# Where an engine reads its ids, and the order of the last scalings, in a gated adapter with layer norm

## The chip, the cores and the metric

The kernel runs on one core of one Trainium2 chip. The metric is the device time of one execution in microseconds (us); the number that counts is the median of a few executions. TensorE (PE), VectorE (DVE), ScalarE (ACT), GpSimd (POOL) and SyncE (SP) each work through an instruction list of their own, in order. SP issues almost all DMA transfers here.

## The reference

Each of 128 batches holds a matrix x of 128 rows and 512 columns in float32 and one id from 0 to 8 (the tables have ten rows). The id picks a small network out of ten, and the result is added to x:

```
h   = relu(x @ W1[id] + b1[id])               # 128x512 @ 512x128
y   = x + h @ W2[id] + b2[id]                 # 128x128 @ 128x512
n   = (y - mean(y)) / sqrt(var(y) + 1e-5)     # per row of 512
out = x + n * gamma[id] + beta[id]
```

The ids are known only on the chip, so every table address depends on a value that an engine has to read into one of its registers.

## The kernel before, in words

One batch is one tile of 128x512, and all 128 batches go through the same steps, about seven of them in flight at once. For batch b:

- SP loads x two batches at a time (`load_x`, L188) and stores the result two at a time (`store`, L632). The tables W1 (as 128x512 tiles), W2, and the broadcast rows of beta, gamma and b2 stay in SBUF. The early batches load their W1 from HBM (`load_first`, L326); from batch 17 on ACT mostly copies it in SBUF (`stage_w1`, L481), and some batches load it (`load_rows`, L453, `load_late`, L742).
- PE transposes x in four blocks (`transpose_x`, L490), ACT copies the result to SBUF (`copy_xT`, L494), PE multiplies with W1 (`down`, L513, eight matmul records), ACT applies the relu (`relu`, L521), PE multiplies with W2 (`up`, L535, two records).
- GpSimd makes x + b2 (`add_b2`, L500) and x + beta (`add_beta`, L507). DVE adds x + b2 to the product and sums the rows (`residual`, L553); ACT squares and sums (`square`, L576), forms the negative mean (`scalar_means`, L567) and the root (`deviation`, L586); DVE refines the root in three small steps (`rstd`, L590, L592, L595), multiplies y - mean by gamma (`scale`, L619) and ends with times rstd plus x + beta (`finish`, L628).

The order on each engine is written out. After a written-out opening, a list `plan` holds every step of the middle with a position: the batch number plus an offset out of the tables `STEPS`. The list is sorted by position and issued; `keep` chains the instructions of one engine in that order. A position one higher is about 2.2 us later. Behind the plan stands a closing list, written out step by step, for the last batches: with E = 123, E+2, E+3 and E+4 are batches 125, 126 and 127.

**Reading ids.** `read_ids` (L271) issues one register read (TENSOR_LOAD in the profile) that brings a few ids from an SBUF row into registers of one engine. The ids of the first 20 batches (`NEAR`) lie unpacked in `lang` and are read four at a time (`near`); the other 108 lie packed, four batches to a word, in the 27 words of `packed`, read four words at a time and three the last time (`far`). A group is read once per engine, at the first call that needs it; later calls use the registers. GpSimd reads all 27 packed words in one go (`far_at_once`, called at L793). Before the change, PE reads groups 0 and 4 of `lang` in the opening (L773); the other reads stand in the plan as steps of their own:

- `lid` of batch b+5 on ACT and PE and of b+6 on GpSimd, at position b+0.99 (L819 to L822); only the first call for a group reads;
- on DVE group b+4 behind the scaling of every fourth batch (L865);
- the seven groups of `packed` on ACT, PE and DVE at 6.5, 6.3 and 7.0 and every two positions after that (L869 to L871), so the last ones stand at 18.5, 18.3 and 19.0.

SP reads its groups where it needs them, and that is not touched.

**The closing list.** For the last five batches the steps are taken apart: `mean_of` (L670 on ACT), `square_of` (L688), `root_of` (L586), `rstd_of` (L590, L592, L595), `scale` (L619) or `scale_out` (L719, the same product into another tile), `end_of` (L713, the last sum), and for batch 125 a sum on PE: `diag_of` (L729 on ACT), `product_of` (L734), `copy_out` (L737 on ACT). `store_last` (L745 on SP) stores single batches and halves; SP takes them in the order of the list.

Of the kernel before, what the change touches and what calls it, by code (L numbers as in the profile page):

```python
# [13 lines left out]
ET = mybir.EngineType  # L14
# [3 lines left out]
G = 4  # L18
# [125 lines left out]
def cond_resid_kernel(ctx: ExitStack, tc: tile.TileContext, x, itok, W1, b1, W2, b2, gamma, beta, out):  # L144
# [8 lines left out]
    nc = tc.nc  # L153
# [9 lines left out]
    def keep(ins):  # L163

        engine = ins.ins.engine
        if engine in last:
            tc.add_manual_dep(ins.ins, last[engine], behind, reason="kept order")
        last[engine] = ins.ins.name
        return ins
# [14 lines left out]
    E = B - 5  # L184
# [70 lines left out]
    NEAR, BITS = 20, 5  # L255
    FAR = (B - NEAR) // 4
# [13 lines left out]
    def read_ids(tile, engine, most, why):  # L270
        loads, vals = nc.values_load_multi_w_load_instructions(  # L271
            tile, engines=[engine], min_val=0, max_val=most, skip_runtime_bounds_check_because=why
        )
        for ins in loads:
            keep(ins)
        return vals

    def near(b, engine):
        g = b // G
        if (g, engine) not in lids:  # L280
            lids[g, engine] = read_ids(
                lang[0:1, g * G : (g + 1) * G], engine, L - 1, "clamped on the chip to 0..L-1 above"
            )
        return lids[g, engine][b % G]
# [13 lines left out]
    def far_at_once(engine):  # L298
        vals = read_ids(packed, engine, ((1 << 4 * BITS) - 1) * H, "four ids of 0..L-1 at five bits each, times H")
        for i in range(0, FAR, G):  # L300
            lids[(NEAR + i) // G, engine] = vals[i : i + G]
# [200 lines left out]
    def add_beta(b):  # L502
        g, j = divmod(b, 2)
        if g not in os:
            os[g] = op.tile([P, 2, H], FP, tag="o", name=f"o_{g}")
        v = lid_h(b, ET.Pool)
        keep(nc.gpsimd.tensor_tensor(os[g][:, j, :], xb(b), beta_b[:, bass.ds(v, H)], ALU.add))  # L507
# [108 lines left out]
    def scale(b):  # L616
        v = lid_h(b, ET.DVE)
        keep(
            nc.vector.scalar_tensor_tensor(  # L619
                ys[b], ys[b], col(nmeans, b), gamma_b[:, bass.ds(v, H)], ALU.add, ALU.mult  # L620
            )
        )
# [43 lines left out]
    def mean_of(b, engine):  # L666
        if b // 2 not in nmeans:
            nmeans[b // 2] = st.tile([P, 2], FP, tag="nmean", name=f"nmean_{b // 2}")
        if engine is nc.scalar:
            keep(nc.scalar.activation(col(nmeans, b), col(sums, b), AF.Copy, scale=-1.0 / H))  # L670
        else:
            keep(
                nc.vector.scalar_tensor_tensor(  # L673
                    col(nmeans, b), col(sums, b), -1.0 / H, ys[b][:, 0:1], ALU.mult, ALU.bypass
                )
            )
# [4 lines left out]
    def add_of(b, cols=slice(0, H)):  # L681
        o = out_of(b)[:, cols]
        keep(nc.gpsimd.tensor_tensor(o, rs[b][:, cols], o, ALU.add))

    def square_of(b):
        ssqs[-b] = st.tile([P, 1], FP, tag="ssq", name=f"ssq_of_{b}")
        sq = tp.tile([P, H], FP, tag="sq", name=f"sq_{b}", bufs=1)
        keep(nc.scalar.activation(sq, ys[b], AF.Square, bias=col(sums, b), scale=-float(H), accum_out=ssqs[-b]))  # L688
# [6 lines left out]
    def rstd_of(b, n):  # L695
        t, u = parts_of[-b]
        if n < 3:
            newton(n, ssqs[-b], t, u)
        else:
            rstds[-b] = st.tile([P, 1], FP, tag="rstd", name=f"rstd_of_{b}")  # L700
            newton_3(rstds[-b], t, u)
# [3 lines left out]
    def base_of(b, pool, tag):  # L705
        base[b] = pool.tile([P, H], FP, tag=tag, name=f"base_{b}")
        pick_b = pick[:, bass.ds(lid(b, ET.PE), 1)].to_broadcast([96, P])
        keep(nc.tensor.matmul(base[b], lhsT=pick_b, rhs=parts[:96, :], start=True, stop=False))
        keep(nc.tensor.matmul(base[b], lhsT=ident, rhs=xb(b), start=False, stop=True))

    def end_of(b, cols=slice(0, H)):
        o = out_of(b)[:, cols]
        keep(nc.vector.scalar_tensor_tensor(o, (rs if b in base else ys)[b][:, cols], rstd_col(b), base[b][:, cols] if b in base else o, ALU.mult, ALU.add))  # L713

    def scale_out(b):
        v = lid_h(b, ET.DVE)
        rs[b] = rp.tile([P, H], FP, tag="r", name=f"n_{b}")
        keep(
            nc.vector.scalar_tensor_tensor(  # L719
                rs[b], ys[b], col(nmeans, b), gamma_b[:, bass.ds(v, H)], ALU.add, ALU.mult  # L720
            )
        )
# [3 lines left out]
    def diag_of(b, engine):  # L726
        diags[b] = st.tile([P, P], FP, tag="diag", name=f"diag_{b}", bufs=2)
        if engine is nc.scalar:
            keep(nc.scalar.activation(diags[b], ident, AF.Identity, scale=rstd_col(b)))  # L729
        else:  # L730
            keep(nc.vector.tensor_scalar(diags[b], ident, rstd_col(b), None, ALU.mult))
# [12 lines left out]
    def store_last(b, engine=nc.sync, cols=slice(0, H)):  # L744
        keep(engine.dma_start(out=out[b][:, cols], in_=os[b // 2][:, b % 2, cols]))  # L745
# [45 lines left out]
    spread(18, nc.scalar)  # L791
    spread(19, nc.scalar)
    far_at_once(ET.Pool)  # L793
    add_beta(0)
    add_beta(1)
    spread(20, nc.scalar)
# [13 lines left out]
    def at(when, step, *args):  # L810
        plan.append((when, len(plan), step, args))

    def when(name, b):
        return b + of(STEPS[name], b)

    for b in range(B):
        if b >= 20 and b % X == 0:
            at(b + X_STEPS[b // X - 10], load_x, b // X)
        if b >= 3:  # L819
            for n, engine in ((b + 5, ET.Activation), (b + 5, ET.PE), (b + 6, ET.Pool)):  # L820
                if n < NEAR:
                    at(b + 0.99, lid, n, engine)  # L822
        if turn(b) in "Fw":
            at(when("load", b), load_rows if turn(b) == "F" else load_late, b)
        if turn(b) == "F":
            at(when("load", b), load_blocks, b)
            at(when("turn", b), turn_blocks, b)
        elif 5 <= b <= E - 2:
            at(when("transpose", b), transpose_x, b)
            at(when("copy", b), copy_xT, b)  # L830
        if 4 <= b <= E - 3:
            if b2_on_gpsimd(b):
                at(when("r", b), add_b2, b)
            at(when("beta", b), add_beta, b)
            at(when("down", b), down, b)
            at(when("relu", b), relu, b)
        if seeded(b):
            at(when("seed", b), seed, b)
        if FIRST <= b <= E - 1 and turn(b) not in "Fw":
            at(when("w1", b), stage_w1, b)  # L840
        if 2 <= b <= E - 4:
            at(when("up", b), up, b)
# [4 lines left out]
    def at_pair(g, key, step, *args):  # L847
        if g < E // 2 - 3 or (step, *args) in begun:
            at(key, step, *args)

    for g in range(E // 2 - 1):
        b = 2 * g
        for n in (b, b + 1):
            if b2_by_vector(n):
                at_pair(g, when("vb2", n), vector_b2, n)
            at_pair(g, when("stat", n), residual, n)
            at_pair(g, when("square", n), square, n)
        at_pair(g, when("means", b), scalar_means, g)
        at_pair(g, when("root", b), deviation, g)
        for n in (1, 2, 3):  # L860
            at_pair(g, when(f"n{n}", b), rstd, g, n)
        for n in (b, b + 1):
            at_pair(g, when("scale", n), scale, n)
            at_pair(g, when("end", n), finish, n)
        if b % G == 0 and b + G < NEAR:  # L865
            at_pair(g, when("scale", b) + 0.001, lid, b + G, ET.DVE)
        at_pair(g, when("store", b), store, g)

    for n in range(0, FAR, G):  # L869
        for engine, first in ((ET.Activation, 6.5), (ET.PE, 6.3), (ET.DVE, 7.0)):  # L870
            at(first + n / 2, far, NEAR + n, engine)  # L871

    for _, _, step, args in sorted(plan, key=lambda step: step[:2]):
        step(*args)
# [119 lines left out]
    root_of(E + 3)  # L994
    rstd_of(E + 2, 3)
    square_of(E + 4)
    diag_of(E + 2, nc.scalar)
    scale_out(E + 2)
    base_of(E + 2, p_y, "y")
    root_of(E + 4)  # L1000
    mean_of(E + 4, nc.scalar)
    rstd_of(E + 3, 1)
    base_of(E + 4, p_y, "y")
    rstd_of(E + 3, 2)
    add_of(E + 1, halves[0])
    rstd_of(E + 3, 3)
    product_of(E + 2)
    store_last(E + 1, nc.sync, halves[1])
    scale(E + 3)
    rstd_of(E + 4, 1)  # L1010
    store_last(E + 1, nc.sync, halves[0])
    end_of(E + 3)
    rstd_of(E + 4, 2)
    rstd_of(E + 4, 3)
    copy_out(E + 2)
    scale_out(E + 4)
    store_last(E + 3, nc.sync)
    end_of(E + 4, halves[1])
    store_last(E + 2, nc.sync)
# [40 lines left out]
```

## Time and profile before

| | |
|---|---|
| time, median of 3 executions | 301.47 us (300.65, 301.47, 301.47) |
| the profiled execution, own time | 300.83 us |
| its span, first to last instruction | 299.1 us |
| granted TensorE clock | 0.996 |
| busy share of the span: PE, DVE, ACT, POOL | 97%, 97%, 91%, 92% |
| HBM read and written | 51.71 MB and 33.55 MB, 285 GB/s over the span |

Times in the rows count from the first instruction of the span. A row of the timeline begins with start and duration in us, then engine, line, operation, tiles and the number of merged instructions; in square brackets stands the idle time of the engine before it and what ended it. An engine with a q behind its name (PEldq, DVEq, SPq) is the engine's sequencer: register reads, semaphore waits and DMA issues stand there and do not count as busy. A row of a source line gives the shortest, median and longest duration in ns and the first and last start in us.

### The profile page before, as it was taken

What the parts mean: (1) busy time and instruction counts of PE and PEld (TensorE: products, weight loads), DVE (VectorE), ACT (ScalarE), POOL (GpSimd) and SP (SyncE); (2) the same over time, 40 slices, a digit from 0 to 9 for tenths busy, and PEclk for the clock granted to TensorE, in tenths of its full rate; (3) what the DMA queues carried; (4) which work ended last, traced back from release to release, by engine and by line L of the source; (5) the groups of instructions that cost most, each with busy time, mean ns of one, the idle gap of its engine ahead of it and who ended that gap; (6) DMA issues with size and microseconds to landing.
All of it is one profiled execution on the core that took longest, in us unless ns stands there. A gap on an engine that the chain in (4) does not pass through costs nothing. (4 is left out here: it accounts for less than half of the span.)

```text
span 299.1 us, 8487 instructions
## 1 busy us (share of the span) xinstructions
PE 290.8 (97%) x1779; PEld 216.3 (72%) x1779; DVE 288.9 (97%) x780; ACT 273.4 (91%) x760; POOL 276.3 (92%) x238
## 2 busy tenths in 40 slices
PE   7999998999999999999999999999999999999992
PEld 3868776777777777777777777777777777777760
DVE  6999998999999999999999999999999999999995
ACT  4877886999999999999999999999999999899992
POOL 1199998998999999999999999999999999999982
PEclk9999999999999999999999999999999999999998
DMA  6999999989487997869995997859976898993816
GB/s 228 384 388 369 343 312 407 360 287 286 168 279 245 312 390 229 317 206 345 323 301 179 276 403 249 323 191 328 346 226 253 277 355 265 307 346 121 272 50 234
DMA packets 62260, 85.82 MB, mean 287 GB/s; under 512 B 4185, under 2 KB 26212, under 8 KB 62210
## 3 DMA queue, kind: packets, MB, share of 16 engines
q1 hardware_dynamic: 62150, 85.23, 83.8%
q8 instruction: 16, 0.26, 0.4%
q14 instruction: 34, 0.28, 0.3%
q10 hardware_dynamic: 60, 0.05, 0.1%
HBM read 51.71 MB, written 33.55 MB: 285 GB/s over the span
## 5 line engine op out<-in xcount | busy, mean ns | idle before, releaser
L507 POOL TENSOR_TENSOR o<-x,beta_b 128x512 f32<-128x512 f32 x121 | 153.6, 1304 | 12.6 <-DVE beta_b L408 12.6
L513 PEld LDWEIGHTS ph<-xT,w1s 128*128 128x128 f32 x1024 | 126.9, 192 | 15.1 <-ACT hT L521 9.1
L513 PE MATMUL ph<-xT,w1s 128*128 128x128 f32 x1024 | 135.7, 275 | 1.2 <-ACT sq L576 1.1
L500 POOL TENSOR_TENSOR r<-x,b_b 128x512 f32<-128x512 f32 x83 | 106.7, 1305 | 2.9 <-DVE part L592 2.2
L535 PE MATMUL py<-w,hT 128*128 x196 | 100.5, 595 | 0.0
L490 PEld LDWEIGHTS pxT<-ident,x 128*128 128x128 f32 x464 | 60.2, 151 | 52.5 <-issue 38.0
L619 DVE SCALAR_TENSOR_TENSOR py<-py,nmean,gamma_b 128x512 f32<-128x512 f32 x124 | 92.5, 751 | 0.3
L576 ACT ACTIVATE sq<-py,sum 128x512 f32<-128x512 f32 x124 | 86.1, 694 | 2.8 <-DVE py L553 1.0
L628 DVE SCALAR_TENSOR_TENSOR o<-py,rstd,o 128x512 f32<-128x512 f32 x116 | 84.9, 746 | 2.7 <-issue 1.5
L494 ACT COPY xT<-pxT 128x512 f32<-128x512 f32 x116 | 68.3, 588 | 7.9 <-PE pxT L490 6.5
L490 PE MATMUL pxT<-ident,x 128*128 128x128 f32 x464 | 71.3, 277 | 0.1
L553 DVE SCALAR_TENSOR_TENSOR py<-py,r 128x512 f32<-128x512 f32 x88 | 60.7, 690 | 0.0
L521 ACT ACTIVATE hT<-ph,b1T 128x128 f32<-128x128 f32 x128 | 47.7, 373 | 4.8 <-PE ph L513 2.4
L481 ACT COPY w1s<-w 128x512 f32 x80 | 48.7, 622 | 0.2
L535 PEld LDWEIGHTS py<-w,hT 128*128 128x128 f32 x196 | 30.1, 192 | 1.8 <-issue 1.1
L527 PE MATMUL py<-w,hT 128*128 x60 | 30.8, 595 | 0.0
L576 ACT ACTIVATION_READ_ACCUMULATOR sq<-py,sum 128x1 f32 x124 | 25.9, 209 | 0.0
L553 DVE SCALAR_TENSOR_TENSOR py<-py,b_b 128x512 f32<-128x512 f32 x30 | 20.6, 687 | 0.0
L473 ACT COPY py<-x 128x512 f32<-128x512 f32 x30 | 18.0, 599 | 0.2 <-DVE o L628 0.2
L586 ACT ACTIVATE root<-ssq,eps 128x2 f32<-128x2 f32 x62 | 16.9, 273 | 0.5
L567 ACT ACTIVATE nmean<-sum 128x2 f32<-128x2 f32 x61 | 13.0, 213 | 0.3 <-DVE rstd L595 0.2
L553 DVE DVE_READ_ACCUMULATOR py<-py,r 128x1 f32 x88 | 12.3, 139 | 0.0
(83 smaller groups left out, 152.9 us busy)
## 6 DMA issues: line engine op xcount, KB each, us to landing
x<-in_x_dram SPq DMA_DIRECT2D x64, 512.0 KB, 7.3
out_dram<-o SPq DMA_DIRECT2D x62, 512.0 KB, 6.7
w1s<-in_L_cond_W_dram SPq DMA_DIRECT2D x25, 256.0 KB, 7.3
w1s<-in_L_cond_W_dram SPq DMA_DIRECT2D x48, 64.0 KB, 4.1
x<-in_x_dram SPq DMA_DIRECT2D x48, 64.0 KB, 2.0
w<-in_L_cond_W_dram SPq DMA_DIRECT2D x4, 640.0 KB, 8.1
w<-in_L_cond_W_dram SPq DMA_DIRECT2D x1, 1792.0 KB, 9.9
w<-in_L_cond_W_dram SPq DMA_DIRECT2D x1, 768.0 KB, 5.3
```

The source lines that it names most:

```text
L481: keep(nc.gpsimd.tensor_copy(dst, src) if gpsimd else nc.scalar.copy(dst, src))
L490: keep(nc.tensor.transpose(pxs[b][:, k, :], cols, ident))
L494: keep(nc.scalar.copy(xT[b], pxs.pop(b)))
L500: keep(nc.gpsimd.tensor_tensor(rs[b], xb(b), b2_b[:, bass.ds(v, H)], ALU.add))
L507: keep(nc.gpsimd.tensor_tensor(os[g][:, j, :], xb(b), beta_b[:, bass.ds(v, H)], ALU.add))
L513: nc.tensor.matmul(phs[b], lhsT=w1s[b][:, k, :], rhs=xT_of(b, k), start=(k == 0), stop=(k == KC - 1))
L521: keep(nc.scalar.activation(hT[b], phs.pop(b), AF.Relu, bias=b1T[:, bass.ds(lid(b, ET.Activation), 1)]))
L535: keep(nc.tensor.matmul(ys[b], lhsT=hT[b], rhs=w2[:, bass.ds(v, H)], start=not m, stop=True))
L553: nc.vector.scalar_tensor_tensor(ys[b], ys[b], 1.0, r, ALU.mult, ALU.add, accum_out=sum_of(b))
L576: nc.scalar.activation(sq, ys[b], AF.Square, bias=col(sums, b), scale=-float(H), accum_out=col(ssqs, b))
L619: nc.vector.scalar_tensor_tensor(ys[b], ys[b], col(nmeans, b), gamma_b[:, bass.ds(v, H)], ALU.add, ALU.mult)
L628: nc.vector.scalar_tensor_tensor(o, ys[b], rstds[g][:, j : j + 1], o, ALU.mult, ALU.add)
```

## The change

The reads of ids move. GpSimd reads its five groups of `lang` right behind the packed words, in the opening. On ACT, PE and DVE the eleven groups behind the first stand in one row in the plan, from positions 3.9, 3.7 and 4.1 on, 0.55 apart, so the last ones stand at 9.4, 9.2 and 9.6. The three sets of read steps in the plan go away. The number of reads on each engine stays.

In the closing list the negative mean of batch 127 (ACT) moves ahead of the diagonal of batch 125, directly behind the square of 127; the scaling of 126 (DVE) moves ahead of the three root steps of 126; the scaling of 127 (DVE) moves ahead of the second root step of 126 and of all those of 127; and the three root steps of 126 and 127 are interleaved ahead of the last sum of 126.

```diff
@@ opening @@
     far_at_once(ET.Pool)
+    for n in range(0, NEAR, G):
+        near(n, ET.Pool)
     add_beta(0)
@@ plan, for b in range(B) @@
-        if b >= 3:
-            for n, engine in ((b + 5, ET.Activation), (b + 5, ET.PE), (b + 6, ET.Pool)):
-                if n < NEAR:
-                    at(b + 0.99, lid, n, engine)
@@ plan, for g in range(E // 2 - 1) @@
-        if b % G == 0 and b + G < NEAR:
-            at_pair(g, when("scale", b) + 0.001, lid, b + G, ET.DVE)
         at_pair(g, when("store", b), store, g)
 
-    for n in range(0, FAR, G):
-        for engine, first in ((ET.Activation, 6.5), (ET.PE, 6.3), (ET.DVE, 7.0)):
-            at(first + n / 2, far, NEAR + n, engine)
+    reads = [(near, n) for n in range(0, NEAR, G)] + [(far, NEAR + n) for n in range(0, FAR, G)]
+    for n, (read, b) in enumerate(reads[1:]):
+        for engine, first in ((ET.Activation, 3.9), (ET.PE, 3.7), (ET.DVE, 4.1)):
+            at(first + n * 0.55, read, b, engine)
@@ closing list @@
     square_of(E + 4)
+    mean_of(E + 4, nc.scalar)
     diag_of(E + 2, nc.scalar)
     scale_out(E + 2)
     base_of(E + 2, p_y, "y")
     root_of(E + 4)
-    mean_of(E + 4, nc.scalar)
+    scale(E + 3)
     rstd_of(E + 3, 1)
     base_of(E + 4, p_y, "y")
+    scale_out(E + 4)
     rstd_of(E + 3, 2)
     add_of(E + 1, halves[0])
+    rstd_of(E + 4, 1)
     rstd_of(E + 3, 3)
     product_of(E + 2)
     store_last(E + 1, nc.sync, halves[1])
-    scale(E + 3)
-    rstd_of(E + 4, 1)
+    rstd_of(E + 4, 2)
     store_last(E + 1, nc.sync, halves[0])
+    rstd_of(E + 4, 3)
     end_of(E + 3)
-    rstd_of(E + 4, 2)
-    rstd_of(E + 4, 3)
     copy_out(E + 2)
-    scale_out(E + 4)
     store_last(E + 3, nc.sync)
     end_of(E + 4, halves[1])
     store_last(E + 2, nc.sync)
```

## The prediction

> **What bounds the kernel now.** I read the page first, then the busy time by stretches, then the waits, then the reads of ids by their own source line, which the page leaves out because register reads do not count as busy.
>
> ```profile
> 18.00:31.00 13.00, 12.93 (x78) 9.82 (x77) 12.28 (x30) 9.90 (x29) 13.00 (x11) 1.00 1.07 370
> 43.00:53.00 10.00, 8.84 (x54) 6.13 (x53) 8.46 (x23) 7.41 (x20) 8.91 (x8) 1.00 1.05 390
> 53.00:278.00 225.00, 224.90 (x1422) 170.54 (x1420) 223.80 (x593) 219.56 (x619) 223.14 (x188) 1.00 0.84 282
> ```
>
> Each row gives a stretch, its length, and the busy time of PE, PE's weight loads, DVE, ACT and GpSimd. From 53 to 278 us PE idles 0.10 us of 225, DVE 1.20, GpSimd 1.86, ACT 5.4: nothing there can make up for lost time, since three engines are full at once. So time lost before 53 us should still be missing at 278, and time saved should still be saved. The one stretch with a hole is 43 to 53: PE, DVE and GpSimd each lose over 1 us. The timeline of that hole, engine by engine:
>
> ```profile
> 49.33 0.60 PE L490 MATMUL pxT<-ident,x 128*128 128x128 f32 x4
> 51.02 1.13 PE L513 MATMUL ph<-xT,w1s 128*128 128x128 f32 x8 [1.08 <-ACT sq L576]
> 49.20 0.37 ACT L521 ACTIVATE hT<-ph,b1T 128x128 f32<-128x128 f32 x1
> 49.97 0.69 ACT L576 ACTIVATE sq<-py,sum 128x512 f32<-128x512 f32 x1
> 52.03 0.59 ACT L494 COPY xT<-pxT 128x512 f32<-128x512 f32 x1 [1.28 <-issue]
> 50.32 0.69 DVE L553 SCALAR_TENSOR_TENSOR py<-py,r 128x512 f32<-128x512 f32 x1
> 52.54 0.75 DVE L628 SCALAR_TENSOR_TENSOR o<-py,rstd,o 128x512 f32<-128x512 f32 x1 [1.47 <-issue]
> ```
>
> PE's wait is put down to ACT's square, which the matmul of L513 doesn't use. The last thing that it uses, the relu that frees its bank, ended at 49.20 + 0.37 = 49.57. By the plan, the step that stands at each of the three holes is the last read of packed ids: on PE between the transposes and L513 (position 18.3), on ACT between the square and the copy (18.5), on DVE between the residual and the finish (19.0). The source line of the reads, first from 17 to 43 us, then from 43 to 53:
>
> ```profile
> L271 PEldq TENSOR_LOAD <-packed x5: 329/330/333, 22.1 to 39.5; - x5
> L271 ACTq TENSOR_LOAD <-packed x5: 305/310/310, 23.3 to 39.4; - x5
> L271 DVEq TENSOR_LOAD <-packed x5: 338/342/351, 24.4 to 41.1; - x5
> L271 DVEq TENSOR_LOAD <-lang x4: 340/374/598, 18.6 to 40.7; - x4
> ...
> L271 PEldq TENSOR_LOAD <-packed x2: 1253/1686/2119, 43.3 to 48.8; - x2
> L271 ACTq TENSOR_LOAD <-packed x2: 997/1631/2265, 44.2 to 49.7; - x2
> L271 DVEq TENSOR_LOAD <-packed x2: 885/1554/2224, 47.7 to 50.2; - x2
> L271 DVEq TENSOR_LOAD <-lang x1: 789/789/789, 49.2 to 49.2; - x1
> ```
>
> From 17 to 41 us the fifteen reads of packed ids take 0.31 to 0.35 us, and those of `lang` on DVE 0.37 in the middle (its first 0.60); the seven reads behind 43 us take 0.79 to 2.27. The last read on PE starts at 48.8 and takes 2.12, so it ends at 50.96, and L513 starts at 51.02; on ACT and DVE the read ends 0.1 us ahead of the next instruction as well. So the holes are slow reads. What makes them slow, the rows show only by its time: SP's first result store is issued in between.
>
> ```profile
> 40.91 0.41 SPq L632 DMA_DIRECT2D out_dram<-o  x1
> ```
>
> **The change part by part.**
>
> *The reads leave the slow stretch.* Their new positions, 3.7 to 9.6, lie between PE's transposes of batch 5 (3.90) and the matmul of batch 8 (9.09), which the rows below have at 20.49 and 29.38; so the last read falls near 30 us, over 10 us ahead of the first store, where the rows above have reads of 0.33. PE's L513 could then start when the transposes have issued. Normal pitches:
>
> ```profile
> 20.49 0.64 PE L490 MATMUL pxT<-ident,x 128*128 128x128 f32 x4
> ...
> 27.16 1.06 PE L513 MATMUL ph<-xT,w1s 128*128 128x128 f32 x8
> 28.05 1.02 PE L535 MATMUL py<-w,hT 128*128 x2
> 28.91 0.64 PE L490 MATMUL pxT<-ident,x 128*128 128x128 f32 x4
> 29.38 1.06 PE L513 MATMUL ph<-xT,w1s 128*128 128x128 f32 x8
> ...
> 43.69 1.02 PE L535 MATMUL py<-w,hT 128*128 x2
> 44.80 1.13 PE L513 MATMUL ph<-xT,w1s 128*128 128x128 f32 x8
> ```
>
> The pitch from transposes to L513 is 0.47 (28.91 to 29.38), so L513 comes at 49.33 + 0.47 = 49.80 instead of 51.02: 1.22 us. The first slow PE read, at 43.3, makes the pitch behind L535 1.11 instead of 0.86: 0.25 more. Together PE gets 1.47. DVE would start its finish at about 50.98 instead of 52.54, 1.56, and ACT gets 1.28. Late next are PE and ACT about equally; ACT has 5.4 us of idle time in the next stretch and takes the smaller number without harm. I take 1.4 for the steady stretch; the ends are 1.2 (the large hole on PE alone) and 1.56 (DVE's).
>
> *The reads arrive in a full stretch.* From 18 to 31 us PE is at 12.93 of 13 and DVE at 12.28, and by about 30 us five reads more on PE and eight more on DVE run there than before. Each takes 0.33 to 0.34 on the sequencer, which runs ahead of the engine: the read costs nothing while the instruction in front still works. PE's pieces between two reads are 0.47, 0.89 or 0.86 long, DVE's large ones 0.69 and more; the shortest cover is longer than a read. Only on DVE do two reads stand behind one instruction (0.68 against 0.69 of a residual). If the cover is gone, a read costs at most its own 0.34; for eight that is 2.7 us. The nearest rows are the reads of the same stretch, around which PE lost 0.07 us in all, so I take 0.1, between 0 and 2.7.
>
> The Trainium skill, "DMA: Bandwidth & Descriptors", section "Latency and other measured facts", speaks against this move: it gives a register load (`tensor_load`) a floor of about 600 ns. By that floor the ten reads on PE would not fit under a cover of 0.47 us, and the sum would be 1.3 us worse; the rows here have 0.33 and disagree with it.
>
> *GpSimd.* Four reads of 0.32 move from behind running adds to the opening, where GpSimd waits for the beta rows. It reads the first group at 9.5, so the four more end near 11, and its first add starts at 14.07.
>
> ```profile
> L271 POOLq TENSOR_LOAD <-lang x5: 322/324/343, 9.5 to 31.3; - x5
> ...
> 14.07 4.98 POOL L507 TENSOR_TENSOR o<-x,beta_b 128x512 f32<-128x512 f32 x4 [12.60 <-DVE beta_b L408]
> ...
> 69.62 1.27 POOL L500 TENSOR_TENSOR r<-x,b_b 128x512 f32<-128x512 f32 x1 [1.13 <-DVE part L592]
> ```
>
> They cost nothing under the 12.6 us of idle time, and gain nothing, as the adds in front hid them. If GpSimd were the bound, the saving would die in it, because it idles only 1.86 us behind 53. But 1.13 of these are one wait on DVE, at 69.62, which shrinks by what DVE gains, so GpSimd can follow by 1.13; the other 0.3 has to come out of its lead, and the view of waits behind 53 has no row in which DVE or PE waits for GpSimd.
>
> *The closing list.*
>
> ```profile
> 291.27 0.75 DVE L719 SCALAR_TENSOR_TENSOR n<-py,nmean,gamma_b 128x512 f32<-128x512 f32 x1
> 292.23 0.39 ACT L729 ACTIVATE diag<-ident,rstd_of 128x128 f32<-128x128 f32 x1
> 291.93 0.16 DVE L590 SCALAR_TENSOR_TENSOR part_of<-ssq_of,root_of 128x1 f32<-128x1 f32 x1
> 292.59 0.76 DVE L619 SCALAR_TENSOR_TENSOR py<-py,nmean,gamma_b 128x512 f32<-128x512 f32 x1
> 292.71 0.19 ACT L670 ACTIVATE nmean<-sum 128x1 f32<-128x1 f32 x1
> 293.38 0.75 DVE L713 SCALAR_TENSOR_TENSOR o<-py,rstd_of,o 128x512 f32<-128x512 f32 x1
> 294.50 0.75 DVE L719 SCALAR_TENSOR_TENSOR n<-py,nmean,gamma_b 128x512 f32<-128x512 f32 x1
> 295.37 0.87 DVE L713 SCALAR_TENSOR_TENSOR o<-n,rstd_of,base 128x256 f32<-128x256 f32 x2
> 294.16 0.33 SPq L745 DMA_DIRECT2D out_dram<-o  x1
> 296.30 0.38 SPq L745 DMA_DIRECT2D out_dram<-o  x1
> DMA to landing us min/median/max: 1.9/2.0/2.7
> ```
>
> On the old clock: the scaling of 126 can start behind L719 of 125, at 291.93 instead of 292.59; one root step; the scaling of 127 at about 292.66 instead of 294.50 (its mean takes the diagonal's place at 292.23 and is there at 292.4 instead of 292.9); five small steps, some 0.19 apart where they depend on each other, to 293.9; the last sum of 126 at 293.9 instead of 293.38, later by 0.5; the two halves of 127 from 294.56 instead of 295.37, earlier by 0.8. ACT's diagonal starts 0.1 later, and the sum of 125 with it. The end is a store, and SP issues them in order: 126 at about 294.68 instead of 294.16, then 125, then the halves, about 0.42 to 0.47 apart. The last issue comes at about 296.0 instead of 296.30. So of 0.8 on DVE the late start of 126's store eats most; 0.3 is left at the issue. The store of 126, 256 KB, now lands nearer to the others, so I take 0.25; the ends are -0.2 (the four stores share one stretch of transfer) and 0.8 (DVE's gain in full).
>
> *Sum:* 1.4 - 0.1 + 0.25 = 1.55, from the profiled execution's 300.83 (span 299.1, and 1.7 around it): 299.3. This execution is 0.64 under the median of the three runs, 301.47; for half of that I add 0.3: **299.6**.
>
> **The rivals.** *The saving dies in a full engine.* GpSimd is 99% busy behind 53, and if its wait at 69.62 doesn't shrink, DVE runs into it, and only the tail and a part of the hole is left: about 300.4. For it speaks GpSimd's 13.00 of 13.00 from 18 to 31 and 223.14 of 225.00 behind 53; against it, that the waits name no engine that waits for it behind 53.
>
> *The reads stay slow where they go.* The rows tie slowness to the time behind 41 us, not to the store. If full DMA queues make it, the early stretch, where the DMA share is 1.07 as against 1.05 in the hole, could have slow reads too. At 0.60, the longest read there so far, PE's ten reads would outlast their shortest cover of 0.47 by 0.13 each, 1.3 in all, and most of the saving would be gone: 299.6 + 1.3 = 300.9. This is also the case in which the change does not do what it says. Against it stand the fifteen reads at 0.31 to 0.35. The Trainium skill's floor of 600 ns leads to the same time.
>
> *Slower: uncovered reads.* It decides itself at a cover shorter than 0.34 us. If DVE's eight more reads all stood in the open, 2.7 us would be lost before 31 us and never made up: 300.83 - 1.4 - 0.25 + 2.7 = 301.9, and 302 with the runs' median.
>
> *More than forecast.* If DVE's hole and all of the tail on DVE count, 1.56 + 0.8 = 2.4 is saved: 298.5.
>
> **How the numbers follow.** Forecast 0.66, more 0.08, dies in an engine 0.14, slow reads early 0.07, uncovered reads 0.05. A measurement of this kernel can tell about 0.3% from no change, which is 0.9 us, so the line lies at 300.57. Faster: 0.66 + 0.08 + a fifth of the third case = 0.77; within: 0.18; slower: 0.05. The range goes from 298.6, near the largest saving, to 300.9, which takes in the case of a full engine and the early slow reads.
>
> **What would show it.** Right: all reads of PE, ACT and DVE end by 31 us and take about 0.33; no idle time by issue near 50 us; the wait of GpSimd near 69 is gone or shrunk; L619 and both L719 at the end stand in a row, and the last issue of SP is about 1.6 us earlier. Wrong: reads over 0.5 us in the new place, new idle time on PE or DVE between 18 and 31 us, a wait of DVE's residual on GpSimd behind 70, or a last store that lands no earlier than the shift of the middle.

## The result and the profile after

The changed kernel takes **299.90 us**, the median of five executions (299.81 to 300.21); the kernel before takes 301.09 (five executions, 300.65 to 301.47, the three above among them). The ratio is 0.9965, with a 95% interval of 0.9952 to 0.9977: faster by 0.35%, or about 1.05 us. The profiled execution of the changed kernel is the longest of its five (300.21 us, span 298.4); the spans of the other four are 298.0 to 298.1.

Lines up to 793 are the same in both kernels. The busy time by stretches of the changed kernel, with the columns as before (PE, PE's weight loads, DVE, ACT, GpSimd, then the granted clock, the DMA share and GB/s):

```profile
18.00:31.00 13.00, 12.90 (x77) 9.84 (x76) 11.21 (x28) 9.87 (x29) 13.00 (x12) 1.00 1.07 372
43.00:53.00 10.00, 9.99 (x65) 7.63 (x64) 9.89 (x26) 8.94 (x28) 7.49 (x7) 1.00 1.05 392
53.00:278.00 225.00, 224.92 (x1420) 170.36 (x1419) 223.82 (x594) 219.87 (x619) 224.52 (x189) 1.00 0.84 284
```

The hole between 43 and 53 us is gone: PE has 9.99 of 10 us there, where it had 8.84, and DVE 9.89 instead of 8.46. In return DVE does less between 18 and 31 us, 11.21 instead of 12.28; a part of that, 0.60, it had done by 18 us already (15.72 instead of 15.12). Behind 53 us PE and DVE are as full as they were. The place of the old hole on the timeline of PE and of DVE:

```profile
49.93 0.60 PE L490 MATMUL pxT<-ident,x 128*128 128x128 f32 x4
50.37 1.06 PE L513 MATMUL ph<-xT,w1s 128*128 128x128 f32 x8
```

```profile
50.97 0.69 DVE L553 SCALAR_TENSOR_TENSOR py<-py,r 128x512 f32<-128x512 f32 x1
...
51.58 0.75 DVE L628 SCALAR_TENSOR_TENSOR o<-py,rstd,o 128x512 f32<-128x512 f32 x1
```

On PE the matmul of L513 follows the transposes by 0.44 us instead of 1.69. On DVE the finish follows the residual by 0.61 instead of 2.22. The same two DVE rows give the whole balance: the residual stands at 50.97, **0.65 later** than before (50.32), and the finish at 51.58, **0.96 earlier** than before (52.54). So, on DVE, the hole was worth 1.61 us, and 0.65 had been lost ahead of it.

Where it was lost is seen on DVE between 22 and 25 us. First the kernel before, then the changed one:

```profile
22.43 0.70 DVE L553 SCALAR_TENSOR_TENSOR py<-py,x 128x512 f32<-128x512 f32 x1
...
23.04 0.15 DVE L590 SCALAR_TENSOR_TENSOR part<-ssq,root 128x2 f32<-128x2 f32 x1
...
23.97 0.16 DVE L595 SCALAR_TENSOR_TENSOR rstd<-part,root 128x2 f32<-128x2 f32 x1
24.24 0.75 DVE L628 SCALAR_TENSOR_TENSOR o<-py,rstd,o 128x512 f32<-128x512 f32 x1
```

```profile
22.48 0.70 DVE L553 SCALAR_TENSOR_TENSOR py<-py,x 128x512 f32<-128x512 f32 x1
...
23.36 0.16 DVE L590 SCALAR_TENSOR_TENSOR part<-ssq,root 128x2 f32<-128x2 f32 x1
...
24.36 0.16 DVE L595 SCALAR_TENSOR_TENSOR rstd<-part,root 128x2 f32<-128x2 f32 x1
24.88 0.75 DVE L628 SCALAR_TENSOR_TENSOR o<-py,rstd,o 128x512 f32<-128x512 f32 x1 [0.37 <-DVE rstd L595]
```

The reads that DVE's sequencer makes in the two gaps, from the source line of the reads in narrow windows (shortest, median and longest in ns, first and last start in us):

```profile
L271 DVEq TENSOR_LOAD <-lang x2: 343/346/349, 22.5 to 22.9; - x2
...
L271 DVEq TENSOR_LOAD <-packed x1: 341/341/341, 24.4 to 24.4; - x1
```

Two reads of 0.35 stand behind the one residual of 22.48; the step after it comes 0.88 later instead of 0.61, so 0.27 is lost. One read stands behind the root step L595, which runs 0.16 us; the finish comes 0.52 after it instead of 0.27: 0.25 more. The other 0.13 of the 0.65 is in pieces below 0.1. That the reads cause the two delays is an argument from their place here; the kernel with covered reads, below, tests it. Neither of these reads is slow. The reads of packed ids on the three engines from 17 to 43 us, and those of `lang` on DVE:

```profile
L271 PEldq TENSOR_LOAD <-packed x7: 331/332/769, 21.9 to 28.9; - x7
L271 ACTq TENSOR_LOAD <-packed x7: 304/308/761, 22.1 to 29.9; - x7
L271 DVEq TENSOR_LOAD <-packed x7: 338/339/751, 24.4 to 30.4; - x7
L271 DVEq TENSOR_LOAD <-lang x5: 340/349/594, 18.7 to 23.6; - x5
```

Apart from DVE's first read of `lang` (0.59, and 0.60 in the kernel before), only the last of each engine, the one of three words, took 0.75 to 0.77, though it has fewer words than the others. The reads of `lang` on PE and ACT in this stretch, not shown, take 0.31 to 0.34.

GpSimd followed. Its wait for DVE now comes once, at 50 us, and takes 2.51; behind 53 us its idle time is 0.48 of 225 us, and no row of the waits there has an engine that waits for GpSimd's adds.

```profile
50.38 1.28 POOL L500 TENSOR_TENSOR r<-x,b_b 128x512 f32<-128x512 f32 x1 [2.51 <-DVE part L592]
```

The end, first DVE's last sums (the two halves of batch 127), then two of SP's stores, that of batch 126 and the very last (the first line of each pair is the issue, the second the time from issue to landing):

```profile
293.52 0.86 DVE L713 SCALAR_TENSOR_TENSOR o<-n,rstd_of,base 128x256 f32<-128x256 f32 x2
```

```profile
L745 SPq DMA_DIRECT2D out_dram<-o x1: 794/794/794, 293.6 to 293.6; - x1
DMA to landing us min/median/max: 2.5/2.5/2.5
...
L745 SPq DMA_DIRECT2D out_dram<-o x1: 407/407/407, 295.5 to 295.5; - x1
DMA to landing us min/median/max: 2.1/2.1/2.1
```

DVE ends at 293.52 + 0.86 = 294.38, 1.86 us earlier than before; 0.96 of that is the shift of the middle, 0.90 is the new order. But the last issue comes at 295.5 and lands at 297.6, only 0.6 earlier than before (296.30 + 1.9 = 298.2). In this execution SP's issue of 126's store took 0.79 instead of 0.33, and the next store was issued 0.9 behind it, where the kernel before has 0.4. The other four executions have spans 0.3 to 0.4 shorter, so a part of this late end may belong to this execution alone; they have no trace that could show it.

### The profile page after: what moved, and what is told of

It is laid out like the page before. It is cut to its first block, busy times and chain, and to the rows that moved or that the text cites. A ratio compares the mean times of both kernels' runs of the same rounds, so it can differ in the third digit from the quotient of the medians.

```text
span 298.4 us, 8486 instructions
## 1 busy us (share of the span) xinstructions
PE 289.7 (97%) x1779; PEld 215.3 (72%) x1779; DVE 288.5 (97%) x780; ACT 273.6 (92%) x760; POOL 276.1 (93%) x238
## 5 line engine op out<-in xcount | busy, mean ns | idle before, releaser
L513 PEld LDWEIGHTS ph<-xT,w1s 128*128 128x128 f32 x1024 | 126.7, 192 | 13.7 <-ACT hT L521 8.7
L513 PE MATMUL ph<-xT,w1s 128*128 128x128 f32 x1024 | 135.5, 275 | 0.2
L500 POOL TENSOR_TENSOR r<-x,b_b 128x512 f32<-128x512 f32 x83 | 105.3, 1284 | 3.0 <-DVE part L592 2.5
L490 PEld LDWEIGHTS pxT<-ident,x 128*128 128x128 f32 x464 | 59.6, 151 | 53.3 <-issue 38.5
```

The lines of the kernel that those rows point to most:

```text
L490: keep(nc.tensor.transpose(pxs[b][:, k, :], cols, ident))
L500: keep(nc.gpsimd.tensor_tensor(rs[b], xb(b), b2_b[:, bass.ds(v, H)], ALU.add))
L513: nc.tensor.matmul(phs[b], lhsT=w1s[b][:, k, :], rhs=xT_of(b, k), start=(k == 0), stop=(k == KC - 1))
```

## The experiments

The times are medians in us; the ratio is to runs of the kernel before on the same chip, with its 95% interval. The reads alone, the closing list alone, the covered reads and these with a last read of four words ran beside 17 executions of the kernel before (median 300.79); the 28th word, the loads for stores, the unused probes and both remedies beside 11 (301.01); the used probes beside one. The loads for stores and both kernels with probes ran once each.

**The reads alone, and the closing list alone.** Each kernel is one half of the change.

```diff
 e1_reads_only: the changed kernel with the closing list of before
-    mean_of(E + 4, nc.scalar)
     diag_of(E + 2, nc.scalar)
...
+    mean_of(E + 4, nc.scalar)
...
 e2_closing_only: the kernel before with the changed closing list
+    mean_of(E + 4, nc.scalar)
     diag_of(E + 2, nc.scalar)
...
+    scale(E + 3)
     rstd_of(E + 3, 1)
     base_of(E + 4, p_y, "y")
+    scale_out(E + 4)
...
```

> Only the reads of ids move, the closing list is that of before. Theory (the gain is the hole near 50 us, less what the reads cost DVE before 31 us): the middle of the kernel lies 0.97 us earlier than before, as in the changed kernel, and the end as well: about 300.0 us, ratio to before 0.996 to 0.998. Rival (the closing list carries the gain): within 0.3 us of before, 300.8 to 301.4.

> Only the closing list changes, the reads stay where they were. Theory (DVE ends 0.9 us earlier, but the last sum of batch 126 is later and SP issues the stores in order, so the last landing moves by -0.4 to +0.3 us): 300.7 to 301.3 us, not told from before. Rival (the end of DVE sets the end of the kernel): 0.8 us less, 300.3 us.

| kernel | us | ratio | span |
|---|---|---|---|
| reads alone | 299.89 (299.68 to 300.08) | 0.9972 [0.9961, 0.9983] | 298.1 |
| closing list alone | 301.01 (300.70 to 301.66) | 1.001 [1.0001, 1.0019] | 299.2 |

Both came out as their theories had them. The reads carry the gain, as far as these runs can tell; the closing list has none, and by its interval may cost up to 0.6 us. The reading that follows, of why, rests on one profiled execution of each kernel. It takes DVE's last sums and SP's six last stores in the second kernel, and the DMA strips from 290 to 299 us (forty slices of 0.225 us, tenths of the 16 DMA engines), first of this kernel, then of the kernel before:

```profile
294.59 0.86 DVE L713 SCALAR_TENSOR_TENSOR o<-n,rstd_of,base 128x256 f32<-128x256 f32 x2
```

```profile
L745 SPq DMA_DIRECT2D out_dram<-o x6: 332/380/406, 292.9 to 296.1; - x6
...
DMA to landing us min/median/max: 2.2/2.3/2.3
```

```profile
DMA  0009999999999993296097104999999999200000
```

```profile
DMA  0039999999999971592493899999319797000000
```

DVE ends at 294.59 + 0.86 = 295.45 in this kernel, 0.79 earlier than before, though the middle stood 0.10 later in this execution (L719 of batch 125 at 291.37 instead of 291.27); the last issue is at 296.1, 0.2 earlier. But its store lands 2.2 later, at 298.3, as late as before. In the kernel before, the two full stores of 126 and 125 move until about 296.4, and the strip has a gap from there to about 296.7, ahead of the two halves. In this one the four stores, 0.75 MB, stand in one unbroken stretch from about 295.5 to 297.7. By this reading the end now follows the moment at which the first of them is issued and the transfer of all four; that issue has become later, from 294.16 to 294.7.

**DVE's reads where they are covered.** The changed kernel, with only DVE's eleven reads moved, by up to 1.2 positions, so that each stands alone behind one of DVE's long instructions.

```diff
-        for engine, first in ((ET.Activation, 3.9), (ET.PE, 3.7), (ET.DVE, 4.1)):
+        for engine, first in ((ET.Activation, 3.9), (ET.PE, 3.7)):
             at(first + n * 0.55, read, b, engine)
+        at((4.1, 4.34, 4.4, 5.45, 6.32, 6.5, 7.13, 7.25, 7.66, 7.84, 8.62)[n], read, b, ET.DVE)
```

> The changed kernel with DVE's eleven reads each behind a large instruction of its own: none behind a small root step and no two behind one instruction. Theory (0.26 us of DVE are lost behind the pair of reads at 22.5 and 0.25 behind the read at 24.37 that stands behind a root step): DVE's gap at 24.5 goes, the middle lies 1.5 us earlier than before in place of 0.97, time about 299.3 us. Rival (the early loss is the waiting for W2 or the opening, and any read costs DVE its time): no change, 299.9 us.

Measured: **299.33** (299.08 to 300.02), ratio 0.9953 [0.9940, 0.9967], span 297.4. The reads take what they took. DVE between 23 and 25 us and by stretches:

```profile
24.01 0.16 DVE L595 SCALAR_TENSOR_TENSOR rstd<-part,root 128x2 f32<-128x2 f32 x1
24.28 0.75 DVE L628 SCALAR_TENSOR_TENSOR o<-py,rstd,o 128x512 f32<-128x512 f32 x1
```

```profile
18.00:31.00 13.00, 13.00 (x78) 9.86 (x77) 12.21 (x30) 9.89 (x29) 13.00 (x11) 1.00 1.07 372
```

The finish is at 24.28, as in the kernel before (24.24), and PE and DVE are as full from 18 to 31 us as they were there (12.93 and 12.28). L719 of batch 125 stands at 289.70, 1.57 earlier than in the kernel before (291.27) and 0.59 earlier than in the changed kernel (290.29). So the early loss is gone, as the theory had it, and it was a matter of place, not of the reads' number or length.

**The last read with four words, and with its start on a multiple of four.** The last of the seven packed groups has three words. The first kernel adds to the one above that the last read brings words 23 to 26 (four words off the multiple). The second is the kernel before, with the reads at their old places, and a 28th word, so that the last read brings words 24 to 27.

```diff
 e5_covered_four: on top of e4_covered
-        g = NEAR // G + i // G
+        g, lo = NEAR // G + i // G, min(i // G * G, FAR - G)
...
-                packed[0:1, i // G * G : min(i // G * G + G, FAR)],
+                packed[0:1, lo : lo + G],
...
 e3_padded: on top of the kernel before
-    packed = const.tile([1, FAR], I32, name="packed")
+    packed = const.tile([1, FAR + 1], I32, name="packed")
+    nc.gpsimd.memset(packed, 0)
...
-                packed[0:1, i // G * G : min(i // G * G + G, FAR)],
+                packed[0:1, i // G * G : i // G * G + G],
```

> As the one before, and the last read of packed ids brings four words (23 to 26, one of them read twice) instead of three. Theory (a read of three words takes longer than one of four, 0.75 against 0.33 us at 30 us, but its cover is 0.86 us): the last reads on PE, ACT and DVE take 0.33 us, the time stays at about 299.3 us. Rival (the 0.75 come from the place at 30 us, not from the words): they still take 0.75 us.

> The kernel before, with the packed ids filled up to 28 words, so that the last read on each engine brings four words that begin at a multiple of four; every read stays where it was. Theory (a read of three words, or of four words off a multiple of four, is made of single words, about 0.25 us each, and each part gets slower behind 41 us): the last reads on PE, ACT and DVE take 0.8 to 1.3 us in place of 2.1 to 2.3, DVE's hole near 51 us shrinks from 1.47 to under 0.5 us, time 299.8 to 300.2 us. Rival (the hole is due to its place near 50 us, whatever is read): reads of 2.1 us and 300.8 us as before.

The first is a miss for its theory of the size: its last reads became longer, about 0.25 us for each of four words, where three had taken 0.75. Time 299.38 (299.17 to 299.52), ratio 0.9953 [0.9940, 0.9967], the same as without this edit: PE is busy for 13.00 of 13 us from 18 to 31, so the longer reads opened no gap there.

```profile
L271 PEldq TENSOR_LOAD <-packed x7: 329/333/1003, 22.1 to 29.1; - x7
L271 ACTq TENSOR_LOAD <-packed x7: 305/311/914, 22.4 to 29.8; - x7
L271 DVEq TENSOR_LOAD <-packed x7: 339/344/977, 24.6 to 28.1; - x7
```

The second takes **299.84** (299.29 to 300.23), ratio 0.9955 [0.9941, 0.9968]: as much as the whole change as far as the intervals tell, with no read moved. Its reads between 43 and 53 us and DVE's hole (the lines of this kernel are two higher):

```profile
L273 PEldq TENSOR_LOAD <-packed x2: 957/1091/1225, 43.4 to 48.9; - x2
L273 ACTq TENSOR_LOAD <-packed x2: 640/776/912, 44.3 to 49.8; - x2
L273 DVEq TENSOR_LOAD <-packed x2: 1037/1112/1187, 47.7 to 50.5; - x2
```

```profile
51.79 0.75 DVE L630 SCALAR_TENSOR_TENSOR o<-py,rstd,o 128x512 f32<-128x512 f32 x1 [0.59 <-DVE py L555]
```

The last reads, 2.12 to 2.27 us in the kernel before, take 0.91 to 1.23, as the theory had it: slow still, but about half as long. That a read of four words comes in one piece, and one of three word by word, fits this; the sizes below test it without stores. DVE's gap shrinks from 1.47 to 0.59 and stays a little above the expected 0.5. The rival, reads of 2.1 us whatever is read, falls.

**What makes the reads slow behind 43 us.** The kernel before, with its first eight result stores turned into loads of the same size into the same tiles; the first sixteen batches of the result are left out. The reads stay at their old places.

```diff
     def store(g):
+        if g < 8:
+            keep(nc.sync.dma_start(out=os.pop(g), in_=x[2 * g : 2 * g + 2].rearrange("b s h -> s b h")))
+            return
```

> The kernel before, with its first eight pair stores turned round: each is a load of the same size from the input into the same tile, so that the first sixteen batches of the result are left out. Theory (stores make the reads slow): the reads between 43 and 53 us take 0.31 to 0.35 us, the last ones of three words 0.75, and the hole near 50 us is gone or under 0.3 us. Rival (the amount of DMA traffic makes them slow, whichever way it goes): they take 0.8 to 2.2 us as before.

One execution, 299.5 us, span 297.7. The reads and the busy time between 43 and 53 us:

```profile
L271 PEldq TENSOR_LOAD <-packed x2: 327/552/776, 43.6 to 48.9; - x2
L271 ACTq TENSOR_LOAD <-packed x2: 310/509/708, 44.5 to 50.0; - x2
L271 DVEq TENSOR_LOAD <-packed x2: 344/547/750, 47.9 to 50.1; - x2
L271 DVEq TENSOR_LOAD <-lang x1: 341/341/341, 49.5 to 49.5; - x1
```

```profile
43.00:53.00 10.00, 9.99 (x66) 7.62 (x66) 9.93 (x25) 8.94 (x26) 7.88 (x7) 1.00 1.05 386
```

The DMA engines are as full as before (1.05 of their time, 386 GB/s against 390), but the reads are short again, as early in the kernel, and the hole is gone. So it is the direction, and not the amount: the seven reads were slow while results went out, and are not while as much comes in.

**Sizes of a read.** The changed kernel with fifteen more reads on ACT. In the first version their values were used nowhere; in the second they pick the column of a one-element copy.

```diff
...
+    for first in (10.3, 16.9, 30.3):
+        for n, (lo, words) in enumerate(((0, 1), (0, 2), (0, 3), (0, 4), (2, 4))):
+            at(first + 0.45 * n, probe, lo, words)
```

> The changed kernel with fifteen more reads on ACT, whose values are not used: of one, two, three and four words from a multiple of four, and of four words from word 2, at about 32 us, again near 47 us, and again near 75 us. Theory (single words cost about 0.25 us each, four from a multiple of four come in one piece at 0.31; behind the first store each piece is slower): at 32 us 0.25, 0.5, 0.75, 0.31 and 1.0 us, near 47 us two to three times as much. Rival (the number of words alone counts): four words from word 2 cost as much as four from word 0.

> The changed kernel with fifteen more register reads on ACT, whose values pick the column of a one-element copy, so that they stay in the program: of 1, 2, 3 and 4 words from the start of a group of four, and of 4 words from the middle of one, at positions 10.3, 16.9 and 30.3 (near 32, 47 and 76 us). Theory (four words that begin on a multiple of four are brought in one piece, anything else word by word, about 0.25 us each): 0.3, 0.5, 0.75, 0.31 and 1.0 us near 32 us, ahead of the stores. Rival (a read off the usual size or start costs a fixed amount more): 2, 3 and 4 words off the start all take about the same, 0.7 to 1.0. Behind the first store: by the theory each piece is slowed alike, so one word takes no longer than four aligned ones and three words about three times as long; by the rival that the number of words decides, four aligned ones take longest. The time is above 299.9, by the fifteen copies of about 0.2 us as far as ACT has no idle time for them.

The first is inconclusive: the fifteen reads did not stay in the program. ACT has its seven reads of `packed` as in the changed kernel, and fifteen semaphore instructions of 17 ns in place of the new ones; its time of 299.84 says nothing of sizes.

In the second they are there. Ahead of the first store, for 1, 2, 3 and 4 words from the start of a group and 4 words from its middle, then behind it for 1, 2 and 3 words:

```profile
L271 ACTq TENSOR_LOAD <-packed x1: 292/292/292, 32.0 to 32.0; - x1
...
L271 ACTq TENSOR_LOAD <-packed x1: 509/509/509, 33.2 to 33.2; - x1
...
L271 ACTq TENSOR_LOAD <-packed x1: 702/702/702, 34.1 to 34.1; - x1
...
L271 ACTq TENSOR_LOAD <-packed x1: 312/312/312, 35.6 to 35.6; - x1
...
L271 ACTq TENSOR_LOAD <-packed x1: 921/921/921, 36.7 to 36.7; - x1
...
L271 ACTq TENSOR_LOAD <-packed x1: 662/662/662, 47.8 to 47.8; - x1
...
L271 ACTq TENSOR_LOAD <-packed x1: 1402/1402/1402, 49.1 to 49.1; - x1
...
L271 ACTq TENSOR_LOAD <-packed x1: 1381/1381/1381, 51.1 to 51.1; - x1
```

Ahead of the stores each word costs about 0.2 us behind a first of 0.29, except that four from the start of a group cost about as much as one (0.31). The rival, a fixed price for anything unusual, has two, three and four words off the start alike, and falls. Behind the first store four of the five take two to nearly three times as long: the three shown, and four words from the start of a group, 0.86 at 53.3 us. But two and three words cost the same there, and four words from the middle, at 55.7, take 0.92 as they did ahead of the stores, with the DMA share still at 1.05 and a store under way. So the slowing is uneven from read to read, and neither the theory that each piece is slowed alike nor the rival, that four from the start then take longest, holds. At the third place, from 82 to 90 us, they take 0.29, 1.08, 0.71, 0.31 and 0.92: only the one of two words is slow. It ran from 83.7 on, behind a store issued at 82.5 and with the DMA share at 1.02; the share during the other four was 0 to 0.81. The Trainium skill, "Runtime: NRT & Kernel Launch", section "Instruction fetch mechanics", gives about 200 ns for each register of a register load, which the page describes as coming from HBM. Here, from SBUF, the steps between the first three rows (0.22 and 0.19) agree with it; the fourth row, with four words in 0.312, does not.

The time of this kernel was far off: **308.01** in one execution, beside 302.01 of the kernel before. Fifteen copies of 0.19 us don't make that; the view of waits adds that ACT stood idle for 7.4 us in all just ahead of them, behind the reads and the arithmetic on their values. The last section comes back to this kernel.

**Both remedies together.** The reads early and covered on DVE, the 28th word, the closing list of before.

> The reads moved early as in the changed kernel, DVE's each behind a large instruction of its own, the packed ids filled up to 28 words, and the closing list of before. Theory (early reads are free when each has its cover; the closing list is worth nothing): all reads of PE, ACT and DVE behind their first take 0.31 to 0.35 us, the middle lies 1.6 us earlier than before, time 299.1 to 299.4 us. Rival (the padding or the closing list matters): over 0.3 us away from 299.3 us.

Measured: **299.29** (299.07 to 300.08), ratio 0.9944 [0.9931, 0.9957], span 297.8. The time is as the theory had it, and the reads take 0.31 to 0.35 us but for DVE's first (0.59); the middle lies 1.41 earlier (L719 of batch 125, a line two lower in this kernel, at 289.86), not 1.6. This is the fastest median here, but it can't be told from the 299.33 of the kernel with covered reads alone, so neither the 28th word nor the order of the closing list shows once the reads are covered.

## Why the prediction came out as it did

The forecast was 299.6 in 298.6 to 300.9, the measured median 299.90. The main step was right. Of the three terms the first came out 0.2 larger than forecast, the other two 0.55 and about 0.25 below it; so the time lies in the range, but the saving in the middle is well below the sum.

- **The hole is made of slow reads**: right. With the reads away, or with stores turned into loads, or with the last read in one piece, it goes or shrinks. It was worth 1.61 us on DVE instead of 1.4, a little above the step's own upper end of 1.56. The step took a value between ACT's 1.28 and PE's 1.47, as these two would be late next; both followed DVE all the same.
- **The early reads cost 0.1**: this is the step that failed. The changed kernel lost 0.65 there, within the stated bounds of 0 to 2.7. "The shortest cover is longer than a read" looked only at DVE's large instructions. The plan also puts a read behind a root step of 0.16 us whose successor sets the pace (0.25 lost). And for the two reads behind one residual it compared 0.68 with the residual's duration of 0.69, while DVE's next instruction starts 0.61 after the residual, and the two reads run from 22.5 to about 23.2 (0.27 lost). The kernel with covered reads shows it: the same reads elsewhere leave the finish at 24.28, and 0.6 us is gained. The rival of uncovered reads thus named the right mechanism; what fell was its price, eight reads in the open.
- **GpSimd** follows: right. Its rival would have had DVE or PE wait for GpSimd behind 53 us, and there is no such wait.
- **The reads stay slow early**: fell. The reads of four words between 18 and 31 us take 0.30 to 0.36 with the DMA share at 1.07, apart from DVE's first one (0.59, as before). The moved reads reached a little past the two rows that the step named (20.49 and 29.38), from 19.1 to about 31.1 us. The floor of 600 ns that the prediction quotes from the Trainium skill, "DMA: Bandwidth & Descriptors", section "Latency and other measured facts", does not hold for these reads. The reads of three words, 0.75 to 0.77, are above it, and the prediction did not see that they differ from those of four.
- **The closing list gains 0.25**: wrong. Alone it costs 0 to 0.6 us by its interval; beside the moved reads no difference shows (299.90 with it, 299.89 without, beside 301.09 and 300.79 for the kernel before). The working held up to the last issue: DVE 0.8 earlier (measured 0.79), the store of 126 issued at about 294.68 (294.7), the last issue at about 296.0 (296.1). What failed is the landing: the case at the lower end of the step's own bounds, the four stores in one stretch of transfer, is what the trace of the closing list alone shows, so an earlier last issue landed no earlier.
- **The sum**: 1.4 - 0.1 + 0.25 = 1.55 was forecast. The traces have 1.61 - 0.65 = 0.96 in the middle, and the span of the kernel with the reads alone is shorter by 1.0. The changed kernel's profiled span is shorter by only 0.7, with its late end, and the spans of its other four executions by 1.0 to 1.1. The 0.3 that the forecast added for the median over the profiled execution proved about right: the five executions of the kernel before have a median of 301.09, 0.26 above the profiled 300.83. That the forecast is only 0.3 off owes something to the first term's error, which offsets a part of the other two.
- **The signs that it named**: of those for being wrong, three came. The reads of three words took over 0.5, DVE has a new idle time of 0.37 at 24.88, and the last store landed 0.6 earlier, less than the 0.96 of the middle. The last issue was 0.8 earlier, not 1.6.

## What to carry to other kernels

Here a register read cost nothing where it stood alone behind one of DVE's long instructions, and cost its time behind a small root step. The cover to measure is the pitch, from the start of the instruction in front to the start of the next, and not the duration; so look at the small steps in a dependent chain before you put reads there. Read values in the shape that was quick here, four words from the start of a group of four, and early, before stores begin. At the end of a kernel, check whether the last stores move in one stretch; if they do, work out when the last bytes land from the first issue of that cluster and its size, not from the last issue.

## What the runs showed of the hardware

**Reads and stores.** Stores at a DMA share of about 1.05 stretched a read of four words from 0.31 to 0.35 us to between 0.64 and 1.25; loads at the same share did not (0.31 to 0.34). The Trainium skill, "SBUF — State Buffer", section "Terms", has DMA and engines on separate SBUF ports that cannot conflict. The reads here are of an SBUF row, and they did slow down while results went out; no run shows whether that happens at SBUF or elsewhere, nor which path the two share.

**PE's granted clock after two pauses.** In the kernel with used probes, ACT stood idle for 0.8 to 1.6 us behind most of its added reads near 50 us, and PE waited for ACT. PE's timeline there, then the busy time in short stretches, with the granted clock behind the five engines:

```profile
49.41 1.02 PE L535 MATMUL py<-w,hT 128*128 x2
51.62 0.66 PE L490 MATMUL pxT<-ident,x 128*128 128x128 f32 x4 [1.19 <-ACT xT L494]
53.58 2.07 PE L513 MATMUL ph<-xT,w1s 128*128 128x128 f32 x8 [1.30 <-ACT hT L521]
```

```profile
51.00:53.00 2.00, 0.66 (x4) 0.42 (x4) 2.00 (x5) 1.08 (x3) 2.00 (x3) 0.98 1.05 404
53.00:55.00 2.00, 1.42 (x6) 1.43 (x7) 0.01 (x1) 1.11 (x5) 2.00 (x2) 0.50 1.06 409
```

From 50.43 (49.41 + 1.02) to 53.58 PE did nothing but the four transposes of one batch, 0.66 us. From 53 on the granted clock was 0.50; it was back at 1.00 by 60. The eight matmuls of L513 took 2.07 us there instead of 1.06, and DVE had next to nothing to do for 4 us, from 53 to 57. The kernel before, with one wait of 1.08 in its hole, kept 1.00. The Trainium skill, "TensorE: Matmul & The Clock Gate", section "Part 1: The HAM clock gate", has the clock at half after an idle window of about 3.4 us; here it fell some 2.5 us after PE's last product, and with the transposes in between. That the pauses made the clock fall is a reading of this one case. How much of the 6 us is the halved clock, and how much ACT's idle time, was not tried apart.
